# All four batches stored by channels, two of them by accumulating transfers, and a maximum for the meeting test

## The chip, the cores and the metric

The kernel runs on one core of a Trainium2 chip. The metric is device time in microseconds (us), the median of several runs; a profiled execution of its own gives the trace. The engines named below are TensorE (PE, matrix products), VectorE (DVE), ScalarE (ACT), GpSimd (POOL) and SyncE (SP). Each has its own queue of instructions, worked in order; the engines wait for each other by semaphores. DMA transfers are issued from the queues of SP, ACT or POOL and are carried out by 16 DMA engines.

## The reference

The input x has shape (4, 128, 64, 64): four batches, 128 channels, 4096 positions, in float32. Two layers follow one another.

```
# layer 0: attention over positions, 64 inner channels, residual
x = x + wo @ softmax(k q) v                      # q, k, v = wq x, wk x, wv x
# layer 1: on tokens t = x transposed, (4, 4096, 128)
t = t + causal_attention(layernorm(t))           # this sum is called x2 below
# feed-forward part: batch norm over all tokens, then a recurrence in time
Wx = batchnorm(layernorm(t) @ W.T)
y[s] = sigmoid(Wx[s] + y[s-1] @ V.T)             # y[-1] = 0, 4096 steps
t = t + y
return t transposed back to (4, 128, 64, 64)
```

What matters here is the last line but one: the output is the attention's result x2 plus the states y, and it has the channels ahead of the positions, so every token row has to be turned into a column somewhere.

## The kernel before

**Tiling.** Work goes batch by batch: layer 0 of batch b in four blocks of queries, then layer 1 of the batch in eight blocks `g` of 512 tokens (the order is 1, 0, 2 to 7). Each block is a row of items of two key tiles (scores on TensorE, exponential on ACT, sums of the exponentials on DVE, products with the values on TensorE). A hand-written schedule gives each item a slot; what follows a block is cut into small tasks, which `finish1` yields with the number of slots until the next one is due: `sums`, `first` (denominators, the residual, the moments of the layer norm), `norm`, `second` (the transpose of the normed tokens by a DVE transpose of 32x32 squares and a trip through DRAM), `kept` and `third` (product with W, statistics of the batch norm, copy into `xs` by steps). At most one task of each layer is done per slot. A scheduler may move instructions inside an engine's queue; those given to `pin` (`tc.keep_in_program_order`) keep the order in which the program names them.

**The recurrence in parallel.** The 4096 steps of a batch are split into 256 chains of 16 steps (`STEPS`), which run side by side as the columns of a 128x256 tile (channel by chain). Each chain starts some steps ahead of its first one from a guess; the steps from -9 to -7 use statistics of all blocks but the last (`early_step`), those from -6 on the final ones. After step 15 the end of each chain is compared with the start that the next one had (`meet`); if all differ by little enough, the result stands, and otherwise a branch runs `general_path`, which computes all of it again in order. `flag` carries that decision.

**One step** (`step`) of one batch is a matrix product with V (L1294), a DVE instruction that adds the scaled Wx (L1296, `z`) and a sigmoid on ACT (L1300). Four batches alternate, so that one batch's product runs while another's sigmoid does.

**The output before.** It is in two layouts. Batches 0 and 1 (`BY_C = 2`) go by channels: `kept` stores x2 to the DRAM tile `x2c`, the loads at L1249 bring it back as `xc`, POOL adds the states of each step (L1307), and SP stores the sum (L1309), 256 KB a step. Batches 2 and 3 go by tokens: L872 stores x2 to `x2t`, the loads at L1259 bring it back as `xr` (four of 1024 KB), and `residual` turns four steps of half a batch around on TensorE (L1328), adds them to `xr` on DVE (L1333) and stores 256 KB (L1334). Of the sixteen `residual` groups one is placed in each of the steps 4 to 15, between the batches, and four come after the last step, with the meeting test between them: two products that leave the difference in PSUM, then a square and a square with a sum on ACT, per batch.

**Queues.** SP issues nearly all transfers, in order. POOL does the select of the causal mask, a power for each norm, and at the end the sums. A sum tile has three buffers, so POOL's fourth sum waits for the first one's store.

Of the kernel before, what the change touches and what calls it, by code (L numbers as in the profile page):

```python
# [15 lines left out]
P = 128  # L16
# [5 lines left out]
BY_C = 2  # L22
# [4 lines left out]
def general_path(  # L27
# [14 lines left out]
    out_c: bass.AP,  # L42
    out_t: bass.AP,
# [243 lines left out]
    with tc.tile_pool(name="wx", bufs=1) as wxp, tc.tile_pool(name="fwork", bufs=3) as wk:  # L287
# [28 lines left out]
        with tc.tile_pool(name="ys", bufs=3) as ysp, tc.tile_pool(  # L316
            name="ps_y", bufs=2, space=PSUM
        ) as ps_y, tc.tile_pool(name="ps_o", bufs=2, space=PSUM) as ps_o:

            def preload(kb):  # L320
                wn = wk.tile([P, STEPS, B], F32, tag="wn", name="wn")
                nc.vector.tensor_scalar(wn, wx[:, ts(kb, STEPS), :], scale, shift, ALU.mult, ALU.add)
                ps = ps_y.tile([P, STEPS, B], F32, tag="y", name="y_ps")
                nc.tensor.matmul(ps, lhsT=ident, rhs=wn, start=True, stop=False, skip_group_check=True)
                return ps

            nblk = N // STEPS
            prev = None
            nxt = preload(0)
            for kb in range(nblk):  # L330
                ps = nxt
                y = ysp.tile([P, STEPS, B], F32, tag="y", name="y")
                for t in range(STEPS):
                    if prev is not None:
                        nc.tensor.matmul(
                            ps[:, t, :], lhsT=vf, rhs=prev, start=False, stop=t == STEPS - 1, skip_group_check=True
                        )
                    nc.scalar.activation(y[:, t, :], ps[:, t, :], AF.Sigmoid)
                    prev = y[:, t, :]
                    if t == STEPS // 2 and kb + 1 < nblk:  # L340
                        nxt = preload(kb + 1)
                o = ysp.tile([P, B, STEPS], F32, tag="o", name="o")
                nc.gpsimd.tensor_tensor(o, xs[:, :, ts(kb, STEPS)], y.rearrange("p t b -> p b t"), ALU.add)

                S = out_c.shape[2]
                K = STEPS // S
                for b in range(BY_C):
                    oc = ysp.tile([P, S, K], F32, tag="oc", name="oc")
                    nc.vector.tensor_copy(oc, o[:, b].rearrange("p (k s) -> p s k", s=S))
                    nc.sync.dma_start(out=out_c[b, :, :, ts(kb, K)], in_=oc)  # L350
                op = ps_o.tile([P, B - BY_C, P], F32, tag="o", name="oT_ps")
                for b in range(BY_C, B):
                    nc.tensor.transpose(op[:, b - BY_C, :], o[:, b, :], ident)
                oT = ysp.tile([P, B - BY_C, P], F32, tag="oT", name="oT")
                nc.vector.tensor_copy(oT, op)
                nc.sync.dma_start(out=out_t[:, ts(kb, STEPS), :].rearrange("b n c -> n b c"), in_=oT)
# [4 lines left out]
def fast_path(  # L361
# [15 lines left out]
    out_c: bass.AP,  # L377
    out_t: bass.AP,
# [29 lines left out]

    x2c = dram.tile([BY_C, NB, S, Q, BLK], F32, name="x2c")
    x2t = dram.tile([B - BY_C, N, P], F32, name="x2t")  # L410
# [72 lines left out]
    def affine(mv, pool, name):  # L483
# [5 lines left out]
        nc.gpsimd.tensor_tensor(y, var, mhalf[:, :1], ALU.pow)  # L489
# [7 lines left out]
        return scale, shift, shift_half  # L497

# [9 lines left out]
    with tc.tile_pool(name="batch", bufs=1) as batch, tc.tile_pool(name="rows", bufs=2) as rowp, tc.tile_pool(  # L508
# [231 lines left out]
        def squares(src):  # L740

            sq = wk.tile([P, Q, TPB, S], F32, tag="sqT", name="sqT")
            nc.vector.transpose(out=sq.rearrange("p c j t -> p j c t"), in_=src.rearrange("p j (c r) -> p j c r", r=S))  # L743
            return sq
# [66 lines left out]
        def finish0(b, pair):  # L811
# [7 lines left out]
            def joining(g, op):  # L819
# [7 lines left out]
                def by_channels():  # L827
                    sq = squares(bs[b].xh[:, ts(g, TPB)])
# [28 lines left out]
        def finish1(b, g, turn):  # L857
# [4 lines left out]
            def first():  # L862
# [8 lines left out]
                if b >= BY_C:  # L871
                    nc.sync.dma_start(  # L872
                        out=x2t[b - BY_C, ts(g, BLK)].rearrange("(j p) c -> p j c", p=P),
                        in_=xs[:, b, ts(g, BLK)].rearrange("p (j c) -> p j c", c=P),
                    )
                mem["xh"] = wk.tile([P, TPB, P], F32, tag="xh2", name="xh2")
                mem["of"] = moments(b, g)
                if final:
                    in_range(True)
# [4 lines left out]
            def second():  # L884
                mem["xhT"] = wk.tile([P, BLK], F32, tag="xhT2", name="xhT2")
                if final:
                    early_step(2, WHOLE[1])
# [10 lines left out]
                sq = squares(mem["xh"])  # L898
                by_c = dram2.tile([Q, S, Q, P], F32, tag="by_c", name="by_c")
                for q in range(Q):  # L900
                    nc.sync.dma_start(
                        out=by_c[:, :, q].rearrange("c r k -> r c k"),
                        in_=sq[ts(q, S)].rearrange("r c j t -> r c (j t)"),
                    )
                nc.sync.dma_start(out=mem["xhT"], in_=by_c.rearrange("c r q k -> (c r) (q k)"))

            def kept():

                sq = squares(xs[:, b, ts(g, BLK)].rearrange("p (j c) -> p j c", c=P))
# [7 lines left out]
            def third():  # L917
# [22 lines left out]
                if b == B - 1 and g == NB - 2:  # L940
                    ahead()
                    in_range(False)
                nc.scalar.copy(  # L943
                    to.rearrange("p s (j q u) -> p s j q u", q=Q, j=TPB),
                    wp.rearrange("p (q j u s) -> p s j q u", q=Q, j=TPB, s=STEPS),
                )
# [18 lines left out]
            if b < BY_C:  # L965
                yield 1, kept
# [273 lines left out]
    with tc.tile_pool(name="xr", bufs=1) as xrp, tc.tile_pool(name="y", bufs=2) as yp, tc.tile_pool(  # L1240
# [5 lines left out]
        xc = xrp.tile([P, BY_C, NCH, STEPS], F32, name="xc")  # L1246
        for b in range(BY_C):
            for c in range(Q):
                nc.sync.dma_start(  # L1249
# [3 lines left out]

        HALVES = NCH // P
        by_chunk = lambda t: t.rearrange("b (h q s) c -> b h q s c", q=P, s=STEPS)
        xr = xrp.tile([P, B - BY_C, HALVES, STEPS, P], F32, name="xr")
        for b in range(B - BY_C):
            for h in range(HALVES):
                nc.sync.dma_start(out=xr[:, b, h], in_=by_chunk(x2t)[b, h])  # L1259
# [7 lines left out]
        pair = lambda t: t.rearrange("p (h q) -> p h q", q=P)  # L1267

        assert HALVES * TPB == NB
        early = xrp.tile([P, B - BY_C, TPB, NCH], F32, name="early")
        late = xs.rearrange("p b (r h k q) -> p b k r h q", h=HALVES, r=TPB, q=P)

        def states(b, s):
            if b < BY_C:
                return by_step[:, b, s]
            return pair(early[:, b - BY_C, s]) if s < TPB else late[:, b, s // TPB - 1, s % TPB]

        def step(b, s):

            wx = by_step[:, b, s % STEPS]
            shaped = (lambda t: t) if s < 0 else grid if b < BY_C else pair

            order = pin if s >= TPB else lambda ins: None
# [16 lines left out]
        def add(s):  # L1303

            t = sums.tile([P, BY_C, NCH], F32, tag="sum", name="sum")
            by_grid = lambda t: t.rearrange("p b (g c) -> p b g c", c=CPB)
            ins = nc.gpsimd.tensor_tensor(by_grid(t), by_step[:, :BY_C, s], by_grid(xc[:, :, :, s]), ALU.add)  # L1307
            tc.keep_in_program_order(ins)
            tc.keep_in_program_order(nc.sync.dma_start(out=out_c[:, :, s].rearrange("b c k -> c b k"), in_=t))  # L1309


        gap = xrp.tile([P, B], F32, name="gap")

        def meet(b):
            ps = ps_y.tile([P, NCH], F32, tag=f"y{b}", name="gap_ps")
            shaped = grid if b < BY_C else pair
            pin(nc.tensor.matmul(shaped(ps), lhsT=ident, rhs=prev[b], start=True, stop=False))
            nc.tensor.matmul(ps, lhsT=minus, rhs=start[:, b, 1:], start=False, stop=True)
            sq = yp.tile([P, NCH], F32, tag=f"y{b}", name="sq")
            nc.scalar.activation(sq, ps, AF.Square)  # L1320
            nc.scalar.activation(sq, sq, AF.Square, accum_out=gap[:, b : b + 1])


        def residual(s0, b, h):

            ps = ps_r.tile([P, TPB, P], F32, tag="r", name="yT_ps")
            for j in range(TPB):
                ins = nc.tensor.transpose(ps[:, j], states(b, s0 + j)[:, h], ident)  # L1328
                if not j:
                    pin(ins)  # L1330
            part = ds(s0, TPB)
            t = xr[:, b - BY_C, h, part]
            pin(nc.vector.tensor_tensor(t, t, ps, ALU.add))  # L1333
            pin(nc.sync.dma_start(out=by_chunk(out_t)[b - BY_C, h, :, part], in_=t))  # L1334


        groups = [(s0, b, h) for s0 in range(0, STEPS, TPB) for b in range(BY_C, B) for h in range(HALVES)]
        assert HALVES * (B - BY_C) == TPB
        for s in range(-WARM, STEPS):
            for b in range(B):  # L1340
                step(b, s)
                if b == 1 and s >= TPB:
                    group = groups.pop(0)
                    residual(*group)
            if 0 <= s < STEPS - 1:
                add(s)
        tc.mark_branch_hint_location(BRANCH, "LikelyTaken", engines=mybir.ALL_ENGINES)
        for k, group in enumerate(groups):
            residual(*group)
            if k == 1:  # L1350
                add(STEPS - 1)
            if k:
                meet(k - 1)
        meet(B - 1)
# [4 lines left out]
        def judge():  # L1359
            total = xrp.tile([P, 1], F32, name="total")  # L1360
            tc.keep_in_program_order(nc.vector.tensor_scalar(count[:, :B], gap, TOL**4, None, ALU.is_le))
# [70 lines left out]
```

## Time and profile before

| what | us |
|---|---|
| median of three runs | 2019.46 (2019.28 to 2020.02) |
| the profiled execution, its own time | 2020.46 |
| its span in the trace | 2018.7 |
| last state's sigmoid ends | 2008.75 |
| the flag is written | 2015.36 |
| TensorE busy | 2008.4 (99%) |
| DVE busy | 1455.7 (72%) |
| ACT busy | 975.5 (48%) |
| POOL busy | 139.8 (7%) |

The profile gives, for each engine, the time in which it was busy, and follows back from the last instruction the chain of work that ended last. A line of a timeline has start and duration in us, the engine, the line of the program, the operation, output <- inputs, their shapes, how often it ran, and in brackets how long the engine had been idle before and what ended the wait. `SPq` is a DMA issue on SP's queue. "DMA share" in a window is the mean busy share of the 16 DMA engines, beside what they moved in GB/s. The transfers that the change touches, with the size of one and the median time from issue to landing:

```
x2c<-sqT      x64, 64 KB,   2.3 us
x2t<-xs       x16, 256 KB,  2.3 us
xc<-x2c       x8,  512 KB,  10.9 us
xr<-x2t       x4,  1024 KB, 20.9 us
out_x<-sum    x16, 256 KB,  2.6 us
out_x<-xr     x16, 256 KB,  2.5 us
```

### The profile page before, as it was taken

The numbers are of one execution on the slowest core, as the hardware profiler recorded it, in microseconds if no ns is written. First come the engines' busy times: TensorE is split into PE (matmuls) and PEld (weight loads), VectorE is DVE, ScalarE is ACT, GpSimd is POOL, SyncE is SP. The second block draws the span as 40 slices with busy tenths as digits, with TensorE's granted clock in tenths as the row PEclk, the third lists the DMA queues.
The fourth block names the chain that finished last, engine by engine and source line by source line (L and its number), as shares of the span: only waits on it lengthen the run. The fifth ranks groups of instructions, "written<-read, shape, count | busy, mean of one in ns | idle before, by whom it ended". The sixth has DMA issues, their size and how long they took to land.

```text
span 2018.7 us, 31252 instructions
## 1 busy us (share of the span) xinstructions
PE 2008.4 (99%) x11888; PEld 876.3 (43%) x11888; DVE 1455.7 (72%) x2811; ACT 975.5 (48%) x1057; POOL 139.8 (7%) x238
## 2 busy tenths in 40 slices
PE   9999999999999999999999999999999999999998
PEld 3333354444333345444433334444433333544457
DVE  4799977554789987655588997655478898764568
ACT  4666633333666653333366664333356665333247
POOL 1000011000000001000000001000000000110014
PEclk9999999999999999999999999999999999999999
DMA  3111112220110111330112111231010111120038
GB/s 105 44 33 23 22 33 50 61 53 16 43 49 18 23 23 37 74 69 16 43 21 60 23 19 32 53 79 37 16 43 2 23 22 23 33 53 16 16 78 278
DMA packets 238443, 89.02 MB, mean 44 GB/s; under 512 B 174816, under 2 KB 219360, under 8 KB 237776
## 3 DMA queue, kind: packets, MB, share of 16 engines
q1 hardware_dynamic: 237280, 86.42, 18.1%
q8 instruction: 94, 1.54, 0.3%
q14 instruction: 61, 0.50, 0.1%
q0 software_dynamic: 288, 0.39, 0.1%
q10 hardware_dynamic: 720, 0.16, 0.0%
HBM read 45.84 MB, written 36.89 MB: 41 GB/s over the span
## 4 chain that ended last, share of the span: by engine, by line
PE 97%; DVE 2%; ACT 1%; issue 0%; POOL 0%; POOLq 0%; DVEq 0%; ACTq 0%
PE s_ps L1017 23%; PE acc L1075 22%; PE s_ps L1004 22%; PE acc L1066 22%; PE o_ps L673 1%; PE kr_ps L562 1%; PE r_ps L624 1%; PE wx_ps L938 1%; DVE z L1296 1%; PE v_ps L574 1%; PE o_ps L685 1%; PE y_ps L1294 1%; DVE xr L1333 0%; PE warm_ps L524 0%; ACT xs L1300 0%; ACT p L1011 0%
## 5 line engine op out<-in xcount | busy, mean ns | idle before, releaser
L1046 DVE TENSOR_TENSOR dsum<-dsum,p 128x1024 f32<-128x1024 f32 x692 | 845.4, 1222 | 403.1 <-ACT p L1020 295.3
L1011 ACT ACTIVATE p<-s_ps,nshift 128x1024 f32<-128x1024 f32 x512 | 569.6, 1116 | 312.9 <-PE s_ps L1004 295.5
L1020 ACT ACTIVATE p<-s_ps 128x1024 f32<-128x1024 f32 (+2 forms) x288 | 274.2, 952 | 601.8 <-PE s_ps L1017 576.7
L1066 PE MATMUL acc<-p,v 64*64 64x512 f32 x4096 | 530.0, 589 | 0.0
L1004 PE MATMUL s_ps<-kr,swap 64*64 64x512 f32 x2048 | 524.6, 590 | 1.3 <-ACT p L1011 1.3
L1004 PE MATMUL s_ps<-kr 64*64 64x512 f32 x2048 | 522.3, 590 | 0.0
L1017 PE MATMUL s_ps<-rows,xhT 128*128 128x512 f32 (+3 forms) x1152 | 500.7, 558 | 0.0
L1075 PE MATMUL acc<-p,xh 128*128 128x512 f32 (+3 forms) x1152 | 500.2, 557 | 0.0
L1017 PEld LDWEIGHTS s_ps<-rows,xhT 128*128 128x128 f32 x1152 | 214.9, 190 | 244.8 <-issue 202.9
L1075 PEld LDWEIGHTS acc<-p,xh 128*128 128x128 f32 x1152 | 216.1, 190 | 239.8 <-issue 223.4
L1066 PEld LDWEIGHTS acc<-p,v 64*64 64x64 f32 x4096 | 156.9, 133 | 283.2 <-issue 274.8
L1004 PEld LDWEIGHTS s_ps<-kr,swap 64*64 64x64 f32 x2048 | 141.8, 133 | 145.7 <-issue 136.0
L1004 PEld LDWEIGHTS s_ps<-kr 64*64 64x64 f32 x2048 | 141.5, 133 | 135.6 <-issue 134.1
L713 POOL TENSOR_TENSOR ln_rstd<-ln_var,mhalf 128x4 f32<-128x4 f32 x64 | 69.9, 1092 | 1186.0 <-DVE ln_var L711 1186.0
L1054 DVE TENSOR_TENSOR dsum<-dsum,p 128x256 f32<-128x256 f32 (+1 forms) x120 | 56.2, 501 | 60.0 <-POOL p L1026 60.0
L699 DVE SCALAR_TENSOR_TENSOR xs<-o_ps,recs,xs 128x128 f32<-128x128 f32 x256 | 70.5, 343 | 5.4 <-PE o_ps L685 1.7
L729 DVE TENSOR_SCALAR xh<-xs,ln_mv,ln_rstd 128x128 f32<-128x128 f32 x252 | 70.2, 342 | 1.9
L708 DVE BATCH_NORM_STATS2 ln_st<-xs 128x6 f32<-128x128 f32 x256 | 62.8, 272 | 0.0
L1026 POOL TENSOR_SCALAR_AFFINE_SELECT p<-p 128x128 f32<-128x128 f32 x128 | 34.5, 294 | 351.9 <-ACT p L1020 347.7
L1044 DVE COPY dsum<-p 128x1024 f32<-128x1024 f32 x44 | 30.2, 686 | 24.7 <-ACT p L1020 15.2
L743 DVE STREAM_TRANSPOSE sqT<-xh 128x512 f32<-128x512 f32 x63 | 44.7, 710 | 1.7
L943 ACT COPY xs<-wx_ps 128x512 f32<-128x512 f32 x31 | 18.1, 584 | 50.4 <-DVE stats L939 48.4
(161 smaller groups left out, 898.3 us busy)
## 6 DMA issues: line engine op xcount, KB each, us to landing
xs<-in_xT SPq DMA_DIRECT2D x32, 256.0 KB, 3.2
by_r<-sqT SPq DMA_DIRECT2D x128, 64.0 KB, 2.2
xhT<-by_r SPq DMA_DIRECT2D x128, 64.0 KB, 2.0
by_c<-sqT SPq DMA_DIRECT2D x124, 64.0 KB, 1.8
xhT<-by_c SPq DMA_DIRECT2D x31, 256.0 KB, 2.8
xs<-in_x SPq DMA_DIRECT2D x12, 512.0 KB, 5.4
swap<-kr SPq DMA_DIRECT2D x32, 128.0 KB, 2.3
x2c<-sqT SPq DMA_DIRECT2D x64, 64.0 KB, 2.3
```

The costliest lines, as they stand in the source:

```text
L699: nc.vector.scalar_tensor_tensor(t, in0=op[:, ts(j, P)], scalar=rec[:, j : j + 1], in1=t, op0=ALU.mult, op1=ALU.add)
L708: nc.vector.bn_stats(st[:, j], xs[:, b, ds(g * BLK + j * P, P)])
L713: nc.gpsimd.tensor_tensor(y, var, mhalf, ALU.pow)
L729: nc.vector.tensor_scalar(dst[:, j], xs[:, b, ds(g * BLK + j * P, P)], mv[:, j, 0:1], y[:, j : j + 1], ALU.subtract, ALU.mult)
L1004: nc.tensor.matmul(ps[c * M : c * M + M, ts(r, BLK)], lhsT=keys[:, ts(c, M)], rhs=rows[r], start=True, stop=True,)
L1011: nc.scalar.activation(it.p, ps, AF.Exp, bias=nshift)
L1017: nc.tensor.matmul(ps[:, off : off + n], lhsT=lhsT, rhs=rhs, start=True, stop=True)
L1020: ins = nc.scalar.activation(it.p[:, :off], ps[:, :off], AF.Exp, scale=float(P) ** -0.5)
L1046: nc.vector.tensor_tensor(flat, flat, it.p, ALU.add)
L1054: nc.vector.tensor_tensor(den[:, h, q0:], den[:, h, q0:], it.p[:, o : o + n], ALU.add)
L1066: nc.tensor.matmul(bt.acc[c * M : c * M + M, r], lhsT=bt.v[part, m * TPB + j, h], rhs=it.p[part, ts(c, BLK)], start=it.first, stop=it.last,)
L1075: ins = nc.tensor.matmul(bt.acc[:, 0, q0:], lhsT=bt.xh[:, t], rhs=it.p[:, o : o + n], start=it.first and h == 0, stop=it.last and h == 1,)
```

## The change

All four batches now go by channels. Batches 0 and 1 (`BY_POOL = 2`) stay as they were. For batches 2 and 3, `kept` transposes x2 with DVE and stores it to DRAM (`stored`, the same four stores as for the normed tokens), loads it as one tile by channels, and `third` copies that tile by steps and stores it into the output itself (`placed`, 256 KB in pieces of 128 bytes). So x2 lies in the output before the states are there. At the end, the states of both batches for four steps at a time are added to it in the output by a transfer from POOL with `accum_op=ALU.add` (`accumulate`): after step 4, 8 and 12 for the four steps before, then three steps, then one. The states go into a tile `ys`. The tiles `xr`, `early` and `late`, the groups of `residual` and the stores `x2t` are gone.

For the very last block, x2 is stored by `kept` in the middle of `first`; POOL's queue loads it back, POOL copies it by steps, and SP stores it. The sum of step 15 is done by DVE, one batch at a time. The meeting test takes the largest absolute difference from PSUM by a DVE reduction, and compares it with `TOL` rather than the sum of the fourth powers with `TOL**4`. `in_range` of the last block moves from `first` to `second`; steps are pinned from 14 on instead of from 4; the mark of the branch's hint moves ahead of the steps; the host no longer reorders two layouts. `general_path` stores all batches by channels.

```diff
+    def placed(b, g, copy, to, src):
+
+        ins = copy(*by_steps(to, src))
+        nc.sync.dma_start(out=out[b, :, :, ts(g, CPB)], in_=to)
+        return ins
...
+        def stored(src, name, pinned=False):
+
+            sq, ins = squares(src)
+            if pinned:
+                pin(ins)
+            by_c = dram2.tile([Q, S, Q, P], F32, tag=name, name=name)
+            for q in range(Q):
+                ins = nc.sync.dma_start(
+                    out=by_c[:, :, q].rearrange("c r k -> r c k"),
+                    in_=sq[ts(q, S)].rearrange("r c j t -> r c (j t)"),
+                )
...
-                if b >= BY_C:
-                    nc.sync.dma_start(
-                        out=x2t[b - BY_C, ts(g, BLK)].rearrange("(j p) c -> p j c", p=P),
-                        in_=xs[:, b, ts(g, BLK)].rearrange("p (j c) -> p j c", c=P),
-                    )
                 mem["xh"] = wk.tile([P, TPB, P], F32, tag="xh2", name="xh2")
                 mem["of"] = moments(b, g)
                 if final:
-                    in_range(True)
+                    kept()
...
             def kept():
 
-                sq = squares(xs[:, b, ts(g, BLK)].rearrange("p (j c) -> p j c", c=P))
+                x2 = xs[:, b, ts(g, BLK)].rearrange("p (j c) -> p j c", c=P)
+                if b >= BY_POOL:
+                    by_c = stored(x2, "x2_by_c", final)
+                    if final:
+                        unplaced.append(by_c)
+                    else:
+                        mem["x2"] = wk.tile([P, BLK], F32, tag="vT", name="x2")
+                        nc.sync.dma_start(out=mem["x2"], in_=together_c(by_c))
+                    return
+                sq, _ = squares(x2)
...
+                nc.scalar.copy(*by_steps(to, wp))
+                if b >= BY_POOL:
+                    placed(b, g, nc.scalar.copy, wk.tile([P, STEPS, CPB], F32, tag="sqv", name="x2s"), mem["x2"])
...
-            if b < BY_C:
+            if not final:
                 yield 1, kept
...
+        pin(nc.gpsimd.dma_start(out=last, in_=together_c(unplaced.pop())))
+        pin(placed(B - 1, NB - 1, nc.gpsimd.tensor_copy, xrp.tile([P, STEPS, CPB], F32, name="last_s"), last))
+        ys = xrp.tile([P, B - BY_POOL, STEPS, NCH], F32, name="ys")
...
+        def accumulate(s0, s1):
+
+            pin(
+                nc.gpsimd.dma_start(
+                    out=out[BY_POOL:, :, s0:s1].rearrange("b c s k -> c b (s k)"),
+                    in_=ys[:, :, s0:s1].rearrange("p b s k -> p b (s k)"),
+                    accum_op=ALU.add,
+                )
+            )
...
-            nc.tensor.matmul(ps, lhsT=minus, rhs=start[:, b, 1:], start=False, stop=True)
-            sq = yp.tile([P, NCH], F32, tag=f"y{b}", name="sq")
-            nc.scalar.activation(sq, ps, AF.Square)
-            nc.scalar.activation(sq, sq, AF.Square, accum_out=gap[:, b : b + 1])
+            pin(nc.tensor.matmul(ps, lhsT=minus, rhs=start[:, b, 1:], start=False, stop=True))
+            return ps
...
         for s in range(-WARM, STEPS):
             for b in range(B):
                 step(b, s)
-                if b == 1 and s >= TPB:
-                    group = groups.pop(0)
-                    residual(*group)
             if 0 <= s < STEPS - 1:
-                add(s)
-        for k, group in enumerate(groups):
-            residual(*group)
-            if k == 1:
-                add(STEPS - 1)
-            if k:
-                meet(k - 1)
-        meet(B - 1)
+                add(s, nc.gpsimd, [(0, BY_POOL)])
+                if s % TPB == 0 and s:
+                    accumulate(s - TPB, s)
+        accumulate(STEPS - TPB, STEPS - 1)
+        accumulate(STEPS - 1, STEPS)
+        gaps = [meet(b) for b in range(B)]
+        add(STEPS - 1, nc.vector, [(b, b + 1) for b in range(BY_POOL)])
+        for b in range(B):
+            pin(nc.vector.tensor_reduce(gap[:, b : b + 1], gaps[b], AX.X, ALU.max, apply_absolute_value=True))
```

## The prediction

> **What bounds the kernel now.** I read the page first: the chain that ended last, and the busy times.
>
> ```profile
> PE 2008.4 (99%) x11888; PEld 876.3 (43%) x11888; DVE 1455.7 (72%) x2811; ACT 975.5 (48%) x1057; POOL 139.8 (7%) x238
> PE 97%; DVE 2%; ACT 1%; issue 0%; POOL 0%; POOLq 0%; DVEq 0%; ACTq 0%
> ```
>
> TensorE sets the time almost to the end. So work put under the attention is free while it stays covered, and only the last 65 us can change much. Next I cut out the second layer's attention (first to last L1017) of batches 0, 1 and 2:
>
> ```profile
> 250.90:509.80 258.90, 258.88 (x735) 123.72 (x734) 154.66 (x355) 82.97 (x99) 18.27 (x42) 1.00 0.20 42
> 735.70:994.50 258.80, 258.78 (x735) 123.54 (x733) 154.26 (x355) 82.80 (x99) 18.04 (x41) 1.00 0.21 42
> 1220.40:1479.30 258.90, 258.88 (x735) 123.45 (x733) 150.70 (x348) 82.71 (x99) 19.07 (x41) 1.00 0.18 42
> ```
>
> After start, end and length stand the busy times of PE, weight loads, DVE, ACT, POOL, then clock, DMA share and GB/s. Batches 0 and 1 run `kept` (a DVE transpose and four stores per block), batch 2 does not; all three last 258.8 to 258.9 us.
>
> Then the end, as a timeline of POOL, SP and DVE, and as windows:
>
> ```profile
> 1955.11 4.39 SPq L1249 DMA_DIRECT2D xc<-x2c  x7
> 1959.55 7.20 SPq L1259 DMA_DIRECT2D xr<-x2t  x4
> 1976.75 4.50 POOL L1307 TENSOR_TENSOR sum<-xs,xc 128x512 f32<-128x512 f32 x3 [15.00 <-ACT xs L1300]
> 1988.16 12.05 POOL L1307 TENSOR_TENSOR sum<-xs,xc 128x512 f32<-128x512 f32 x8 [6.91 <-DMA out_x<-sum]
> 1991.49 0.68 DVE L1333 TENSOR_TENSOR xr<-xr,yT_ps 128x512 f32<-128x512 f32 x1
> 1992.09 1.65 DVE L1296 SCALAR_TENSOR_TENSOR z<-xs,all_scale,y_ps 128x256 f32<-128x256 f32 x4
> 2015.21 0.15 DVE L1367 TENSOR_SCALAR flag<-tp 1x1 int32<-1x1 f32 x1 [0.37 <-PE tp L1364]
> ```
>
> ```profile
> 1959.00:1974.00 15.00, 14.77 (x70) 10.64 (x69) 12.77 (x36) 12.73 (x31) 0.55 (x1) 1.00 1.05 208
> 1976.00:1984.00 8.00, 7.75 (x38) 5.61 (x37) 7.45 (x18) 6.99 (x17) 4.50 (x3) 1.00 1.00 413
> 1991.00:2003.00 12.00, 12.00 (x70) 10.62 (x68) 12.00 (x29) 9.68 (x23) 10.84 (x9) 1.00 0.97 340
> 2004.00:2013.00 9.00, 8.42 (x52) 7.27 (x50) 6.87 (x14) 5.92 (x16) 4.95 (x4) 1.00 0.95 339
> ```
>
> Two things stand here. In the last twelve steps DVE (four z and one residual, 12.00 busy of 12.00) sets a pace of about 2.17 us a step. And the 16 DMA engines are full nearly throughout: xc comes at 208 GB/s with share 1.05, xr at 413 GB/s, the output at 340 GB/s with share 0.97.
>
> **The change, part by part**, against the profiled execution: its own time 2020.46, span 2018.7, so 1.8 around it. The median of the three runs, 2019.46, is 1.0 lower; I take the difference in span and add it to the median.
>
> *Under the attention.* Sixteen x2t stores go. Batches 2 and 3 get 16 DVE transposes (16 x 0.70, the L743 row from xs, 11.2 us), 64 stores of 64 KB, 15 loads of 256 KB, 15 ACT copies (like L943, 0.58 each, 8.7 us) and stores into the output. TensorE covers this: batch 2 then has the list of batch 1, whose stretch is no longer, plus 8 copies on an ACT that is busy 83 of 259 us. On SP each block puts six transfers where one was, and the x2 load holds the queue until the four stores have landed (about 2 us, as the xhT load does now); behind it stand by_token and own, wanted slots of 3.43 us later. I take 0; without cover it would be 11.2 us of DVE and 8.7 of ACT.
>
> *The last block.* `third` of block 6 now comes one slot (3.43 us) later, since `kept` took a slot. The scale of the states then ends at 1947.7 instead of 1944.2 and L1054 starts there instead of at 1946.80; DVE had 0.72 idle behind it, so den is some 0.1 late. The transpose of the last x2 (0.70) falls into DVE's 0.83 idle before L501. But the four ops of in_range and the count, which filled gaps, now all stand between L727 and L893: from 1958.11, five ops with dependences of 0.2 us end near 1958.86, where L893 started at 1958.59. Sum +0.1 +0.25: I take +0.35 (0 to 1).
>
> *The steps.* Without the residual the pace is that of the steps before it: L1296 x16 in 7.23 us, 1.81 a step. Twelve steps: 12 x (2.165 - 1.815) = 4.2. The last sigmoid ended at 2008.75 and now ends at 2004.9.
>
> *The flag.* It ended 6.6 us after the last sigmoid (four residuals, then two ACT squares a batch). Now: two matmuls (2 x 0.43), a DVE maximum and the same last 0.9 us. The maximum from PSUM is not in the trace: between 0.43 (L924, 128x256) and 0.69 (L637, 128x512); I take 0.45. Flag at about 2007.2 instead of 2015.36. Ahead of the maxima on DVE stand the two adds of step 15, which need the buffer of sum 12; if that store is late, the flag is.
>
> The mark of the branch hint moves, but the only hint in the trace stands at 0.8 us, and in the order of the built program it stands first on each engine in both kernels: 0.
>
> *POOL.* It needs all of xc. The eight loads now queue behind four stores of the last x2 (transposed at 1956.9, four issues of 0.45, so from 1958.7); one had gone at 1951.64. At 208 GB/s 0.52 MB take 2.5 us, eight take 20.2, and about 3 us of start and landing go with it, as before (1955.11 plus seven loads is 1972.8, POOL started at 1976.75 with x2t between): first add at 1982 (1980 to 1984). Fifteen adds at 1.50 are 22.5 us. An accumulating issue is not in the trace; a plain one on POOL took
>
> ```profile
> 2.59 0.54 POOL L418 DMA_DIRECT2D joint<-in_c_woT  x1
> ```
>
> and 0.54 also for 128x1, so not by bytes. With 256 rows instead of 64 to 128, I bound it by 0.54 and 1.1 and take 0.8. First accumulate issued at 1982 + 5 x 1.50 + 0.8 = 1990.3; if nothing held POOL, the last one would be out at 1982 + 22.5 + 5 x 0.8 = 2008.5, 3.6 us behind the last sigmoid. So POOL is late already. What stands ahead of its adds costs nothing: the load of the last x2 (one issue) and the copy into last_s (128x512, some 1.5 us like a sum) lie between the pow at 1961.20 and 1982. The first accumulate also waits for the store of last_s, which SP issues behind the xc loads; it lands a few us after xc, before 1990.3.
>
> *The transfers.* Reloading xr (4.19 MB at 413 GB/s, 10.2 us) goes, and so do 4.19 MB of output at 340 GB/s, 12.3 us. In come four accumulates' worth of 1.05 MB. Their price is not in the trace. From below, one pass: 2.5 us each at 413 GB/s, 10.2 together. From above, three passes (SBUF read, output read, output written, one after another), 30.5. Each element needs two reads for one write, and the engines at share 1.00 moved one read and one write each at that pace; so I take two passes, 20.3. [...]
>
> From 1990.3: 20.3 + 11 sums (5 to 15) of 0.262 MB at 340 GB/s (8.5) = 28.8, to 2019.1. Landing 1.0 (a sum lands 2.6 after its issue, 0.8 of it data). The engines run dry for a while when POOL waits for one of three sum buffers behind an accumulate and issues the next late: I take 1.5 (0 to 4). So the last transfer lands near 2021.6; from the waits at the end to the end of the span it is 2.5 (2016.4 to 2018.7, and one wait). Span 2024.1, +5.4.
>
> **Forecast:** slower by about 5.5 us, 2025.0: T and the flag come earlier, but the output's accumulates end last. Its own range is 2021 to 2029.
>
> **Rivals.** *One pass, POOL the bound (faster).* If reads and writes of an accumulate overlap, 10.2 + 8.5 us fit easily, and the end is POOL's: last issue 2008.5, data 0.7, landing 1.0, 1.0 for sums that hold it, 2.5: 2013.7, so -5.0: 2014.5. For it: xr ran at 413 where the output ran at 340, so the engines have some spare; against: share is 1.00 either way. It decides when 1.05 MB takes under about 3.3 us.
> *In between, no change.* With 1.5 passes 15.2 + 8.5 from 1990.3 end at 2014.0; with 1.0, 1.5 and 2.5 that is 2019.0, +0.3: 2019.8. For it: reads from SBUF and from the output need not share all of a path.
> *Three passes (slower).* 30.5 + 8.5: 2034.3, +15.6: 2035. For it: nothing shows overlap between read and write of the same bytes; against: plain copies have both at full share.
> *The transfer isn't done as it reads.* If POOL spends 3 us on each accumulate's descriptors, add 14 ends at 1982 + 22.5 + 9, the last issue at 2019.5, and the span at 2023.6, +4.9 at whatever price of data. Against it are the flat 0.54 rows.
> [...]
>
> **How the numbers follow.** Forecast 0.45, one pass 0.25, in between 0.15, three passes 0.10, POOL's descriptors 0.05. Range: the low end lets in most of the one-pass case (2013.5), the high end the dear side of two passes and half of three (2034). Within 0.2% (4.0 us, about what a measurement can tell from no change) lies the case in between and the cheap quarter of the forecast: 0.27. Faster is most of one pass: 0.23. Slower: 0.50.
>
> **What would show it.** Steps at 1.81 us to the end and the last sigmoid near 2005; first POOL add near 1982; flag well ahead of the end; accumulates of 1 MB taking about 5 us and landing last; DMA share near 1 from 1990. Wrong if the accumulates land within 4 us, if POOL starts its adds before 1979, or if the layer-1 stretch of batch 2 grows beyond 259.

## The result, and the profile after

The changed kernel takes 2043.38 us (median of four runs, 2042.74 to 2044.68), the kernel before 2019.45 (four runs, 2019.28 to 2020.02): slower, ratio 1.0119, 95% interval 1.0101 to 1.0136. The forecast was slower by 5.5 us; it is slower by 24. The profiled execution took 2044.68, its span is 2043.0.

The page of the changed kernel, busy times, chain, and one group of its list; the last line is the same group in the kernel before:

```profile
PE 2003.2 (98%) x11824; PEld 862.6 (42%) x11824; DVE 1460.7 (72%) x2817; ACT 988.1 (48%) x1060; POOL 144.0 (7%) x244
PE 95%; ACT 2%; DVE 1%; DMA 1%; issue 1%; POOL 0%; SPq 0%; DVEq 0%; POOLq 0%; ACTq 0%
L1026 PE MATMUL s_ps<-kr 64*64 64x512 f32 x2048 | 523.2, 591 | 8.2 <-ACT p L1033 8.2
L1004 PE MATMUL s_ps<-kr 64*64 64x512 f32 x2048 | 522.3, 590 | 0.0
```

TensorE's share fell by a point, and the group of layer 0's scores has 8.2 us of idle time (in one piece, as the timeline below shows), where the kernel before has none. A cut by layers puts a place to it: layer 0 of batch 3, from the first L1026 to the first L1039, lasts 236.23 us (1478.16 to 1714.39); before it was 225.95. Layer 1 of batch 2, the stretch that the prediction watched, is 258.77 and unchanged. The timeline of ACT, SP and TensorE there, and windows of TensorE's clock (after the window's length stand PE, weight loads, DVE, ACT, POOL, granted clock, DMA share, GB/s):

```profile
1495.43 1.11 ACT L1033 ACTIVATE p<-s_ps,nshift 128x1024 f32<-128x1024 f32 x1 [0.60 <-PE s_ps L1026]
1498.57 1.38 SPq L762 DMA_DIRECT2D x_by_c<-sqT  x3
1503.13 0.34 SPq L930 DMA_DIRECT2D x<-x_by_c  x1
1505.77 1.05 ACT L501 COPY x2s<-x 128x512 f32<-128x512 f32 x1 [9.23 <-DMA x<-x_by_c]
1506.73 2.12 ACT L1033 ACTIVATE p<-s_ps,nshift 128x1024 f32<-128x1024 f32 x2
1507.89 1.12 PE L1026 MATMUL s_ps<-kr 64*64 64x512 f32 x2 [8.24 <-ACT p L1033]
```

```profile
1500.00:1505.00 5.00, 0.00 (x0) 0.00 (x0) 2.04 (x2) 0.00 (x0) 0.00 (x0) 0.98 0.46 124
1505.00:1510.00 5.00, 2.11 (x12) 0.80 (x16) 2.02 (x2) 3.12 (x4) 0.00 (x0) 0.50 0.37 72
1510.00:1515.00 5.00, 5.00 (x44) 1.57 (x40) 2.88 (x3) 2.86 (x3) 0.00 (x0) 0.84 0.00 0
```

ACT finishes an exponential at 1496.54, and the next thing in its queue is the copy of x2 by steps (L501) of batch 2's last block. The tile it copies is loaded only at 1503.13, behind four stores. So ACT stands for 9.23 us with exponentials behind the copy whose scores are ready, TensorE waits for those and stands for 8.24, and comes back at half its clock (0.50 granted from 1505 to 1510): two score products take 1.12 us instead of 0.60. For the other fourteen copies of this kind ACT waited five times, 5.6 us in all, and TensorE didn't stand for those.

The end, as POOL's timeline with two instructions of DVE, and as windows:

```profile
1992.95 7.50 POOL L1319 TENSOR_TENSOR sum<-xs,xc 128x512 f32<-128x512 f32 x5 [10.61 <-DMA out_x<-last_s]
2000.38 1.24 POOL L1325 DMA_DIRECT2D out_x<-ys  x1
2009.70 1.53 POOL L1319 TENSOR_TENSOR sum<-xs,xc 128x512 f32<-128x512 f32 x1 [3.52 <-ACT ys L1310]
2011.17 1.21 POOL L1325 DMA_DIRECT2D out_x<-ys  x1
2022.65 1.51 POOL L1319 TENSOR_TENSOR sum<-xs,xc 128x512 f32<-128x512 f32 x1 [5.77 <-DMA out_x<-sum]
2024.11 1.17 POOL L1325 DMA_DIRECT2D out_x<-ys  x1
2026.73 2.53 DVE L1319 TENSOR_TENSOR sum<-xs,xc 128x256 f32<-128x256 f32 x2 [13.17 <-DMA out_x<-sum]
2027.80 2.85 POOL L1325 DMA_DIRECT2D out_x<-ys  x2
2031.26 0.15 DVE L1367 TENSOR_SCALAR flag<-tp 1x1 int32<-1x1 f32 x1 [0.28 <-PE tp L1364]
```

```profile
1993.00:2001.00 8.00, 8.00 (x37) 5.17 (x35) 7.86 (x19) 7.97 (x19) 8.00 (x6) 1.00 0.39 131
2001.60:2010.40 8.80, 8.56 (x39) 5.76 (x38) 8.22 (x20) 8.36 (x20) 5.28 (x5) 1.00 1.02 229
2010.40:2012.20 1.80, 1.80 (x10) 1.20 (x8) 1.76 (x5) 1.79 (x5) 1.80 (x3) 1.00 0.09 22
2012.20:2020.80 8.60, 4.30 (x20) 3.25 (x18) 1.32 (x3) 1.90 (x5) 4.69 (x4) 0.97 1.03 221
2020.80:2025.20 4.40, 0.00 (x0) 0.00 (x0) 0.00 (x0) 0.00 (x0) 2.55 (x3) 0.50 0.14 48
2025.20:2040.00 14.80, 0.19 (x2) 0.09 (x2) 4.33 (x9) 0.00 (x0) 5.46 (x5) 0.50 1.05 212
```

Last column but one: the DMA engines are full, idle for 1.8, full, nearly idle for 4.4, full. POOL's column says why: an accumulate is issued, POOL adds three sums, then waits for a sum buffer (3.52 us, then 5.77; the name in the first bracket is the one that came last by the profile, but the states were there, and the fourth sum needs the first one's store). Only behind that sum does the next accumulate stand. A transfer is carried out in pieces. Here they are counted by their start in some windows of 3 us, with their size, number and mean time, from the trace of the changed kernel (q0: POOL's queue, the accumulates; q1: SP's, the sums):

```
1998-2001   q1 1024 B x512  48 ns
2004-2007   q0 4096 B x157 329 ns
2007-2010   q0 4096 B  x55 327 ns   q1 1024 B x658  47 ns
2016-2019   q0 4096 B x145 328 ns   q1 1024 B  x39  59 ns
2019-2022   q0 4096 B  x12 327 ns   q1 1024 B x694  46 ns
```

While an accumulate runs, hardly a piece of a sum gets through; they go when it is nearly over.

### The profile page after: what moved, and what is told of

The parts are those of the page before. It is cut to its first block, busy times and chain, and to the rows that moved or that the text cites. A ratio compares the mean times of both kernels' runs of the same rounds, so it can differ in the third digit from the quotient of the medians.

```text
span 2043.0 us, 31256 instructions
## 1 busy us (share of the span) xinstructions
PE 2003.2 (98%) x11824; PEld 862.6 (42%) x11824; DVE 1460.7 (72%) x2817; ACT 988.1 (48%) x1060; POOL 144.0 (7%) x244
## 4 chain that ended last, share of the span: by engine, by line
PE 95%; ACT 2%; DVE 1%; DMA 1%; issue 1%; POOL 0%; SPq 0%; DVEq 0%; POOLq 0%; ACTq 0%
PE s_ps L1039 22%; PE acc L1097 22%; PE s_ps L1026 21%; PE acc L1088 21%; PE o_ps L681 1%; PE r_ps L632 1%; PE kr_ps L570 1%; PE wx_ps L961 1%; PE v_ps L582 1%; PE o_ps L693 1%; ACT xs L1310 1%; ACT ys L1310 1%; DMA out_x<-sum 1%; PE y_ps L1304 1%; ACT p L1033 0%
## 5 line engine op out<-in xcount | busy, mean ns | idle before, releaser
L1026 PE MATMUL s_ps<-kr 64*64 64x512 f32 x2048 | 523.2, 591 | 8.2 <-ACT p L1033 8.2
L1026 PE MATMUL s_ps<-kr,swap 64*64 64x512 f32 x2048 | 525.5, 591 | 1.3 <-ACT p L1033 1.3
L1039 PE MATMUL s_ps<-rows,xhT 128*128 128x512 f32 (+3 forms) x1152 | 500.7, 558 | 0.0
L1039 PEld LDWEIGHTS s_ps<-rows,xhT 128*128 128x128 f32 x1152 | 215.1, 190 | 244.2 <-issue 199.8
L1026 PEld LDWEIGHTS s_ps<-kr,swap 64*64 64x64 f32 x2048 | 141.7, 133 | 146.5 <-issue 136.7
L1026 PEld LDWEIGHTS s_ps<-kr 64*64 64x64 f32 x2048 | 141.3, 133 | 145.6 <-issue 135.3
L966 ACT COPY xs<-wx_ps 128x512 f32<-128x512 f32 x31 | 18.1, 584 | 51.8 <-DVE stats L962 49.8
```

Of the source, the lines that this page charges most:

```text
L1026: nc.tensor.matmul(ps[c * M : c * M + M, ts(r, BLK)], lhsT=keys[:, ts(c, M)], rhs=rows[r], start=True, stop=True,)
L1039: nc.tensor.matmul(ps[:, off : off + n], lhsT=lhsT, rhs=rhs, start=True, stop=True)
```

## The experiments

The theory: two separate losses. One is the wait in ACT's queue. The other is the sums' stores, which stand still under an accumulate, so that POOL waits for a buffer and issues the next accumulate late. Rivals: TensorE waited for SP's transfers or the larger traffic; and the accumulates' own transfer sets the end, whatever POOL does. Each run stands against its own runs of the kernel before, whose medians were 2019.67 to 2019.93.

**The copy of that one block on POOL.** (`turn` is true for the last block of a batch.) In the traces every engine works in the changed kernel's order but for this one copy.

```diff
-placed(b, g, nc.scalar.copy, ...)
+placed(b, g, nc.gpsimd.tensor_copy if turn else nc.scalar.copy, ...)
```

> The copy of x2 by steps of batch 2's last block moves from ACT's queue to POOL's, where nothing is behind it; all else is as in the changed kernel. Theory one (ACT's queue stood still for 9.23 us behind this copy, and TensorE with it): the idle 8.2 us of TensorE near 1500 and the slower clock after it go, everything later moves ahead by 9.0 to 9.6 us, and the end with it: 2033.5 to 2034.5. Theory two (the normed tokens' transfers on SP, or the larger traffic, are what TensorE waits for there): TensorE still stands for several us near 1500, and the time stays over 2040.

Measured 2033.74 (2033.41 to 2033.84; ratio 1.0069, 1.0052 to 1.0086): 9.6 us less. ACT's and POOL's timeline in this run, and a window of it:

```profile
1496.23 1.11 ACT L1033 ACTIVATE p<-s_ps,nshift 128x1024 f32<-128x1024 f32 x1 [0.60 <-PE s_ps L1026]
1498.66 1.11 ACT L1033 ACTIVATE p<-s_ps,nshift 128x1024 f32<-128x1024 f32 x1 [1.32 <-DVE dsum L1068]
1506.71 1.17 POOL L501 COPY x2s<-x 128x512 f32<-128x512 f32 x1 [11.74 <-DMA x<-x_by_c]
```

```profile
1500.00:1505.00 5.00, 5.00 (x53) 1.70 (x45) 4.58 (x5) 3.54 (x4) 0.00 (x0) 1.00 0.48 112
```

The load is as late as it was, and now POOL waits for it 11.74 us with nothing behind. TensorE is busy 5.00 of 5.00 at full clock, layer 0 of batch 3 is back at 225.95, and the last sigmoid ends at 2004.62 instead of 2014.10. Theory one holds; SP's transfers and the traffic are all still there, so theory two falls.

**Twelve buffers for the sums.**

```diff
-name="sums", bufs=3
+name="sums", bufs=12
```

> Twelve buffers for POOL's sums in place of three; all else is as in the changed kernel, so the 9 us near 1500 stay lost. Theory one (the sums' stores stand still under an accumulate, POOL waits for a buffer, and the next accumulate is issued late behind it): POOL's adds follow each other every 1.5 us, the accumulates are issued near 2000, 2007, 2014 and 2017, the 16 DMA engines are busy without a break from 2002, and the some 6.5 us in which they were idle between the accumulates go: 2035 to 2037. Theory two (the accumulates' own transfer sets the end, POOL's waits lie beside it): within 1.5 us of 2043.

Measured 2038.21 (2037.20 to 2040.20; ratio 1.0094, 1.0078 to 1.0111): 5.2 us less. POOL's timeline in this run, and a window of it:

```profile
2000.14 1.23 POOL L1325 DMA_DIRECT2D out_x<-ys  x1
2006.91 1.66 POOL L1325 DMA_DIRECT2D out_x<-ys  x1
2013.64 2.07 POOL L1325 DMA_DIRECT2D out_x<-ys  x1
2017.33 3.75 POOL L1325 DMA_DIRECT2D out_x<-ys  x2
```

```profile
2001.00:2033.00 32.00, 15.12 (x68) 10.42 (x66) 19.80 (x35) 12.30 (x28) 20.08 (x15) 0.79 1.04 231
```

The accumulates leave at the expected times, some 10 us earlier at the last, and the DMA share is 1.04 from 2001 to 2033. The time missed the expectation a little: the median of four is 1.2 above its upper end, and the fastest 0.2. Theory two is further off, by 3.3. The buffers were a cause.

**No accumulates, and plain stores in their place.** The first drops the calls of `accumulate`, so the output lacks the states of batches 2 and 3; the second drops only its operation, so the output there holds the states without x2:

```diff
-                if s % TPB == 0 and s:
-                    accumulate(s - TPB, s)
-        accumulate(STEPS - TPB, STEPS - 1)
-        accumulate(STEPS - 1, STEPS)
```

```diff
-                    accum_op=ALU.add,
```

> No accumulates are issued: the states of batches 2 and 3 are left out of the output. Theory one (accumulates hold up the sums): no add of POOL waits for a buffer, 15 adds of 1.5 us from 1993 end near 2015.5, the sum's store of step 15 lands near 2018, and the end is near 2020.5, some 22 us less than with them, more than the about 20 us that two passes of four megabytes cost by themselves. Theory two (the sums wait for something else, such as SP's queue): POOL still waits 3 to 8 us between adds, and the end is at 2027 or later.

> The accumulates become plain stores of the same bytes on the same queue, so the output of batches 2 and 3 holds the states without x2. Theory one (an accumulate costs two passes, about 320 ns for 4096 bytes and 6 us per megabyte, and starves the sums for as long): packets of 160 to 170 ns, some 3 us per megabyte, POOL waits far less for buffers, and the end is at 2024 to 2030. Theory two (the software queue itself, not the adding, is what holds up the sums): packets take about the same as with the adding, the sums stand still as long, and the end stays over 2037.

Without accumulates: 2025.64 (2024.73 to 2027.24; ratio 1.0031, 1.0018 to 1.0044), 17.7 us less than with them, where some 22 were expected. POOL's timeline:

```profile
1993.00 20.93 POOL L1319 TENSOR_TENSOR sum<-xs,xc 128x512 f32<-128x512 f32 x14 [10.80 <-DMA out_x<-last_s]
2015.25 1.52 POOL L1319 TENSOR_TENSOR sum<-xs,xc 128x512 f32<-128x512 f32 x1 [1.33 <-DMA out_x<-sum]
```

The mechanism was right: POOL waits for a buffer once, 1.33 us. What I had left out is the end behind POOL's adds, from the sum of step 15 over the four maxima to the flag (2019.87) and from there to the end of the span (2023.5).

With plain stores: 2030.76 (two runs, 2030.29 and 2031.24; ratio 1.0054, 1.0034 to 1.0074), 0.8 above the upper end that was expected. So the adding costs 12.6 us of the 17.7. POOL's timeline with them:

```profile
2000.51 0.75 POOL L1325 DMA_DIRECT2D out_x<-ys  x1
2006.34 1.54 POOL L1319 TENSOR_TENSOR sum<-xs,xc 128x512 f32<-128x512 f32 x1 [0.54 <-DMA out_x<-sum]
2007.82 0.74 POOL L1325 DMA_DIRECT2D out_x<-ys  x1
2013.73 1.52 POOL L1319 TENSOR_TENSOR sum<-xs,xc 128x512 f32<-128x512 f32 x1 [0.63 <-DMA out_x<-sum]
```

A piece of 4096 bytes takes 163 to 166 ns in a plain store and 328 as an accumulate: the time of two passes, as the forecast had it, and not of one. The same bytes on the same queue make POOL wait for 0.54 and 0.63 us instead of 3.5 and 5.8. The adding itself adds 0.45 us to the issue (1.2 instead of 0.75).

The standing still is not the adding's alone. By the trace without accumulates, the first piece of a sum starts 0.5 us after its issue. With plain stores, the sum issued at 2002.86 moves its first piece at 2004.92, when the plain store's pieces (2002.3 to 2005.1) run out; in the changed kernel the one issued at 2003.22 moves at 2007.12 (the accumulate's pieces: 2002.3 to 2008.7). So sums stand still under a plain store as well, and this run's theory two has that much right; the adding makes it last more than twice as long, and that is what POOL's three buffers don't cover.

**Both edits together, and both without accumulates.**

> Both edits: the copy on POOL for batch 2's last block, and twelve buffers for the sums. Theory one (the two losses are separate and add up): 9.6 and 5.2 us off the 2043.4 of the changed kernel, 2028.6 (2027 to 2030). Theory two (the waits for buffers grew only because everything was late): no better than 2032.

> The copy on POOL, and no accumulates: the states of batches 2 and 3 are left out of the output. It shows what is left of the change without its two costs. Theory one (each step 0.35 us shorter, and the end set by POOL's fifteen adds from 1983.6): 9.6 us below the 2025.6 of the run without accumulates, 2015 to 2017, some 3 us faster than before. Theory two (the stall hid behind something that sets the end anyway): 2018 to 2021.

Measured 2028.27 (2027.52 to 2028.35; ratio 1.0042, 1.0026 to 1.0059) and 2015.34 (2014.65 to 2015.75; ratio 0.9979, 0.9970 to 0.9989). The losses add up: 2043.4 less 9.6 less 5.2 is 2028.6. And the change without the stall and without any store of those states is 4.3 us faster than the kernel before (2019.67 in these runs): it is the accumulates and the stall that turn the sign, and each does so alone (2033.74 without the stall, 2025.64 without the accumulates).

**The meeting by maxima alone, in the kernel before.**

```diff
-            sq = yp.tile([P, NCH], F32, tag=f"y{b}", name="sq")
-            nc.scalar.activation(sq, ps, AF.Square)
-            nc.scalar.activation(sq, sq, AF.Square, accum_out=gap[:, b : b + 1])
+            nc.vector.tensor_reduce(gap[:, b : b + 1], ps, AX.X, ALU.max, apply_absolute_value=True)
...
-            tc.keep_in_program_order(nc.vector.tensor_scalar(count[:, :B], gap, TOL**4, None, ALU.is_le))
+            tc.keep_in_program_order(nc.vector.tensor_scalar(count[:, :B], gap, TOL, None, ALU.is_le))
```

> The kernel before with the new meeting test alone: the square and the square with a sum on ACT become one DVE maximum per batch. In the kernel before the fourth difference leaves TensorE at 2013.5 and ACT's four pairs end at 2014.44; a maximum of 0.33 us would end at 2013.9, so the flag comes 0.6 us sooner, and the end with it unless the last store lands later: 2018.3 to 2019.8, which can't be told from 2019.75. If the test's form matters more than that, 2017 or less.

Measured 2019.19, ratio 0.9998 (0.9988 to 1.0007): no difference that can be told.

**Can accumulating be made good?** The accumulates were put ahead of the adds (with both edits above):

```diff
+            if s % TPB == TPB - 1 and 0 <= s < STEPS - 1:
+                accumulate(s - TPB + 1, s + 1)
+            if TPB - 1 <= s < STEPS - 1:
+                for k in range(TPB if s == TPB - 1 else 1): add(s if s >= TPB else k, nc.gpsimd, [(0, BY_POOL)])
```

> As the run before it, and the accumulates are put ahead of the adds in POOL's queue: the first one ahead of the first sum instead of behind the fifth. Theory one (the work of the DMA engines behind the xc loads sets the end: four megabytes of accumulates at 6 us and sixteen sums at 0.75 us are some 37 us from near 1982.5 on, and in the 8 us behind the first sum the engines are idle by half because the accumulate waits in POOL's queue): first accumulate issued near 1982 to 1984, the engines busy without a break, span 2020 to 2022.5, time 2022 to 2025, still slower than before. Theory two (POOL's adds or the landing of single accumulates set the end): 2027 or more.

Measured 2026.77 (2026.67 to 2028.30; ratio 1.0039, 1.0024 to 1.0053), between the two theories. The first accumulate left at 1985.07; the sums stood behind it in POOL's queue, and the DMA engines had little to do:

```profile
1984.00:1988.00 4.00, 4.00 (x19) 2.67 (x18) 3.94 (x10) 3.99 (x10) 2.93 (x3) 1.00 0.30 23
```

Then xc's loads were cut otherwise; `kept` transposes with the tile index ahead of the channels and stores to the new layout with four transfers as before. By edit and trace these are eight loads of 512 KB, not the four of 1 MB of which the expectation speaks:

```diff
-    x2c = dram.tile([BY_POOL, NB, S, Q, BLK], F32, name="x2c")
+    x2c = dram.tile([BY_POOL, NB * TPB, P, P], F32, name="x2c")
...
+            for h in range(Q):
+                ins = nc.sync.dma_start(
+                    out=xc[:, b].rearrange("p (j k) s -> p j (k s)", j=NB * TPB)[:, ts(h, NB)],
+                    in_=x2c[b, ts(h, NB)].rearrange("j p n -> p j n"),
+                )
```

> As the run with the accumulates ahead of the adds, and xc comes back otherwise: x2c lies by tiles of 128 tokens with the channels next, and four loads of 1 MB go to all 128 partitions in pieces of 512 bytes, instead of eight loads of 512 KB to 32 partitions in pieces of 2048. The eight loads moved some 205 GB/s with the engines' share at 1.05, while the four xr loads of the kernel before, to 128 partitions, moved 415. Theory one (the number of partitions that a load reaches sets the 20 us that xc takes, and with it the first sum): pieces of 512 bytes at about 30 ns, xc in 13 to 16 us, the first sum near 1977 to 1980 instead of 1985, and the end 4 to 6 us sooner, 2021 to 2023. Theory two (loads from this DRAM tile run at 205 GB/s however they are cut, or the end hangs on the accumulates alone): 2026 to 2028.

> The kernel before with the same layout and loads of xc, and nothing else. There the steps are paced by DVE, not by xc: even with xc and xr landing some 5 us sooner the time stays, 2018.7 to 2020.3. If POOL's late sums set its end after all, 2016 or less.

In the changed kernel 2025.49 (2024.80 to 2026.49; ratio 1.0029, 1.0017 to 1.0040), a miss by 2.5 us; in the kernel before 2019.52, ratio 0.9999 (0.9989 to 1.0009), no difference. The loads did get faster: 263 to 307 GB/s instead of 199 to 235, and the last piece near 1976 instead of 1982. But POOL, with the accumulate at the head of its queue, used little of it: that accumulate waits for the states of step 3, and left 1.8 us sooner than in the run before.

```profile
1983.30 1.26 POOL L1326 DMA_DIRECT2D out_x<-ys  x1 [14.68 <-ACT ys L1311]
1984.09 10.93 POOL L1320 TENSOR_TENSOR sum<-xs,xc 128x512 f32<-128x512 f32 x7
```

So the first three sums were put ahead again, which is the loop of the changed kernel with `accumulate(s - TPB + 1, s + 1)` ahead of `add(s)` at steps 3, 7 and 11:

> As the run before with the wide loads, but the sums of steps 0 to 2 stand ahead of the first accumulate in POOL's queue. There the engines were idle from 1978 to 1984, as POOL stood at the accumulate, which waits for step 3's states (1983.3). Theory one (what is left is the DMA engines' work behind step 3): first sum near 1978, three sums stored before 1984, some 2 us of their work out of the way, POOL 4 us ahead, time 2022.5 to 2024; the accumulates still end last, so even this is slower than before. Theory two (the accumulates alone, one after another from 1984 on, set the end): 2025 to 2026, as without the edit.

```profile
1977.33 4.50 POOL L1320 TENSOR_TENSOR sum<-xs,xc 128x512 f32<-128x512 f32 x3 [8.67 <-ACT xs L1311]
1983.46 1.27 POOL L1326 DMA_DIRECT2D out_x<-ys  x1 [1.63 <-ACT ys L1311]
1984.28 6.47 POOL L1320 TENSOR_TENSOR sum<-xs,xc 128x512 f32<-128x512 f32 x4
2004.68 2.85 POOL L1326 DMA_DIRECT2D out_x<-ys  x2
```

Measured 2021.47 (2020.59 to 2022.26), ratio 1.0008 (0.9998 to 1.0018), 1 us better than expected: within 0.2% of the kernel before, and not ahead of it. From 1985.3, when the first accumulate's pieces start, the DMA engines have no break until near 2018 (share 1.02 to 1.10 in every 4 us from 1988 to 2016), so what is left is their work. No complete version that was run beats the kernel before; only the one that leaves the states of two batches out does.

## Why the prediction was wrong

*Under the attention: "I take 0".* This step failed, and cost 9.6 us, the largest part of the miss. The amounts were right (batch 2's layer 1 is not longer, and with the copy on POOL nothing is lost). But the cover was counted by ACT's busy share (83 of 259 us), and the copy costs not its 1.05 us but its wait. The text named what stands behind the x2 load on SP, and not what stands behind the copy on ACT: exponentials, which feed TensorE. Once per run, at the turn from batch 2 to batch 3, the built order puts it where its load is late. The program names it right behind the copy of W's product (L966) of the same block, which ran at 1716.1; the scheduler moved it ahead of that, to 1505.77. Nothing needed it so early; no run pinned it to its place. None of the three signs named as "wrong if" came: the accumulates of 1 MB took 9.2 us to land (median), POOL's adds didn't start early, and layer 1 of batch 2 stayed at 258.77. The sign watched that stretch, and the loss came in the next one, layer 0 of batch 3.

*The idle time of the DMA engines: "I take 1.5 (0 to 4)".* This term was too small, beyond its own range: 5.2 to 5.5 us by the runs with twelve buffers. The mechanism was named as it came (POOL waits for one of three buffers behind an accumulate and issues the next one late), but the 1.5 was an estimate that wasn't worked out from any row. Measured, POOL waits 3.52 and 5.77 us, each time with the next accumulate behind it, and DVE's sum of step 15 waits 13.17 us for its buffer. A megabyte is 256 pieces of 4096 bytes; on 16 engines they take 5.3 us at 328 ns, and 2.6 at the 163 ns of a plain store. For about as long hardly a piece of a sum got through: the sum issued under the accumulate moved its first piece 4.8 us after the accumulate's first one (2002.3 to 2007.12), and under the plain store it was 2.6 (2002.3 to 2004.92). What makes a sum wait that long was not shown; no run cut the accumulates smaller.

*Price of an accumulate: two passes, 20.3 us.* The factor of two is shown (328 ns to 163), though not that it comes from two reads; the size was low. In the run with both edits all pieces of the accumulates together took 23.4 us of the engines' time (17.6 + 4.2 + 1.6), 3.1 more. *First accumulate out at 1990.3*: 1992.0 with the stall gone, as the first sum came at 1983.3 instead of 1982 and an issue took 1.2 us instead of 0.8. These two (3.1 and 1.7) less the 1.5 of idle time that this run doesn't have are the 3.3 us that remain: 2028.3 less 2025.0. With 5.5 for the buffers and 9.6 for the stall that is the whole miss of 18.4. The sum closes with the forecast's other terms (the sums' 8.5, the landing, the end) taken as they stood; they weren't measured one by one, so that it closes to the tenth is partly luck.

*Right:* the steps (1.81 us each, last sigmoid at 2004.62 with the stall gone, 2004.9 predicted), accumulates that end last, a flag well ahead of them, and that the maxima don't matter. But the flag came at 2031.4 and not 2007.2, held by the buffer, and at 2012.4 even with both edits: the first of DVE's two sums of step 15, which the forecast's flag put at nothing, took 5.98 us there (1.10 in the run without accumulates), and no run shows why. Of the rivals, one pass falls by the plain stores, POOL's descriptors by the 1.2 us rows, three passes by the pieces; the time lay beyond them all, as none had a loss in the attention.

## What to carry to other kernels

An instruction put into the queue of an engine that feeds the bottleneck can cost the time that it waits, not the time that it runs (here 9.23 us for a copy of 1.05); look at what its input needs to arrive, and put it on a queue with nothing behind it. With x2 of batches 2 and 3 added in place, the loads of xr, which had lain ahead of the last states, were gone, and what took their place was traffic behind those states, at 328 ns for a piece of 4096 bytes where a plain store took 163; small stores from another queue stood still meanwhile (3.9 us from issue to first piece instead of 0.5). If the engine that issues big transfers also waits for buffers that those transfers hold up, more buffers are the first thing to try (here 5.2 us).

## What the hardware showed

Eight loads of xc to 32 partitions each moved 205 GB/s with the engines' share at 1.05 (1964 to 1968 in the run with the accumulates ahead of the adds), where loads to all 128 partitions moved 413 at share 1.00 (xr, pieces of 8192 bytes, 1976 to 1984 in the kernel before) and 263 to 307 (pieces of 512 bytes, 1960 to 1976 in the changed kernel with the wide loads). The runs changed the partitions and the size of a piece together, so they don't single out a cause.

A stand of 8.24 us cost 10.3 in the trace (layer 0 of batch 3, 236.23 against 225.95). TensorE came back at half its clock (0.50 from 1505 to 1510), and its score products were back at 0.59 us at 1511.92, 4.0 us after it had started again; half of that, 2.0 us, is the rest. Between the medians of runs with and without the stall it is 9.6 us (three buffers), 9.9 (twelve) and 10.3 (no accumulates).
